# Lattice products cut into 64x64 tiles, two rounds a tile pair, with ordering products and five accumulators

## The chip, the cores and the metric

The kernel runs on one core of a Trainium2 chip. The metric is the device time of one execution in microseconds (us). The reference's work on an input of 32 images with 8 channels of 256x256 is done in one launch.

## What is computed

The reference normalises the input in groups, runs a block of three small networks on it, adds the result to the input, normalises again and adds a quantised 3x3 convolution. Cut to what matters here, the first layer is:

```python
drive = x                                  # normalised input, 8 channels
grid = drive
for _ in range(15):                        # STEPS: the lattice
    mapped = 3.9 * grid * (1.0 - grid)
    local = conv3x3_per_channel(mapped, K_local)
    physics = 0.7 * mapped + 0.3 * local
    grid = 0.85 * physics + 0.15 * drive
cml_out = clip(grid, 0.0001, 0.9999)
h = relu(conv3x3(x, Wp, bp))               # 128 hidden channels
nca_out = sigmoid(conv1x1(h, Wu, bu))
g = sigmoid(conv1x1(relu(conv3x3(concat(x, cml_out, nca_out), Wg1, bg1)), Wg2, bg2))
out = g * cml_out + (1 - g) * nca_out
```

The lattice loop is what the change touches. Each step of it is a 3x3 convolution within a channel, so a step needs the whole plane of the step before, and 15 steps follow each other.

## The kernel before, in words

All images are taken in 8 groups of four. For a group, three pieces of work run in the first layer: the lattice (`lattice`), the hidden network (`nca`), and the gate of the group before (`gate`); the normalisation of the next group (`normalise`) is mixed in as well. After the last group's gate comes the second layer, the quantised convolution (L982 to L1040), which the change leaves alone.

**Layout of the lattice.** A plane of 256x256 is put on 128 partitions as four column phases of 32 rows: partition = 32 x phase + row within the tile. A tile has 32 rows, of which 28 are its own; 9 tiles cover an image, and two images stand side by side in one buffer, so a buffer has 18 tiles, with 64 columns a phase (NJ). The loop over tiles takes 6 at a time, so a step has three tile ranges `i`. Each group of four images makes two buffers, `s` = 0 and 1. There are two layouts, "a" and "b", which differ by a shift of the phases: a step takes one buffer from a to b (65 columns a tile, so products with 390 columns) and the other from b to a (64 columns, 384). They change roles at every step. The buffers are `m_a` and `m_b`; the drive is in `d_a` and `d_b`.

**The product of a step.** For each range `i` and each of the two buffers, three fp32 products with weights of 128 rows and 64 columns (L511) make one accumulator `pt`: two write one half of its partitions each from the buffer's own columns (`own`), and the third adds to the second half's sum what the neighbouring columns give (`beside`, one column aside). The two buffers' products alternate, one writing the low and one the high half of the partitions. The six products of a range are called a tile pair's here: three rounds of two products. Of the three weights of a buffer two hold zeros in one half of their 128 rows, so with the rows cut in halves four blocks of 64x64 hold all that is not zero.

**What follows a product.** VectorE adds the drive (`gt`, L519, which frees the accumulator), and makes `mapped` of the next step (L524), written into the other layout's buffer. GpSimd clears the two outer columns after a step from a to b (L528). After a step from b to a, the halo rows between tiles are copied by DMA (`exchange`, L474 and L475): for the first image after range `i` = 1, for the second after `i` = 2. SyncE issues these, and `background(3)` issues three more DMAs of loads and stores for other channels after each range.

**The other products.** `hidden` (L591) multiplies two row blocks of 48 partitions by 128 columns of weights into two accumulators `ph`, with ScalarE's `h` (L601) reading them. `place` (L608) makes `acc` from `h`. The gate has `pa` (L795) and `pg` (L758).

**Accumulators.** PSUM has eight banks here: `ps_c` has six buffers under the tag "pt", which go round among pt, ph, pg and a few one-column sums, and `ps_a` two for acc and pa. A buffer is waited for when its reader of six requests before hasn't finished.

**Order.** TensorE's order is the program's (`manual_schedule` for PE). `together` (after the definition of `lattice`, `nca` and `gate`) alternates the lattice, which yields a cost of 5.91 after each step, with the others' pieces, by their share of the total costs (T_LATTICE = 8 * 45 * 1.97, T_NCA, T_GATE, T_PREP), so a lattice step is followed by a few pieces of filler. VectorE, ScalarE, GpSimd and SyncE are ordered by a scheduler.

Of the kernel before, what the change touches and what calls it, by code (L numbers as in the profile page):

```python
# [31 lines left out]
F32 = mybir.dt.float32  # L32
# [6 lines left out]
PSUM = bass.MemoryType.PSUM  # L39

P = 128
# [16 lines left out]
NJ = W // 4  # L58
# [55 lines left out]
def kernel(  # L114
# [17 lines left out]
    V, S, G, T = nc.vector, nc.scalar, nc.gpsimd, nc.tensor  # L132
# [13 lines left out]
    lw = cp.tile([P, C, 3, P], F32, name="lw")  # L146
# [6 lines left out]
    qw = cp.tile([P, 3, P], BF16, name="qw")  # L153
# [19 lines left out]
    with tc.tile_pool(name="prep", bufs=1) as pp, tc.tile_pool(name="prep2", bufs=2) as pp2:  # L173
# [24 lines left out]
        for t, n, w in (  # L198
# [3 lines left out]
            k = 64 if w == W else 43  # L202
# [63 lines left out]
    with ExitStack() as one:  # L266
# [4 lines left out]
        pool = lambda name, bufs, **kw: one.enter_context(  # L271
            tc.tile_pool(name=name, bufs=bufs, reuse_waits="tile", **kw)
        )
        hp, xp, sp2, gp, bp2 = pool("hp", 12), pool("xp", 4), pool("sp2", 1), pool("gp", 3), pool("bp2", 2)
        st, imp, wk, wk1, np_ = pool("st", 2), pool("imp", 3), pool("wk", 2), pool("wk1", 2), pool("np", 1)
        ps_c, ps_a = pool("ps_c", 6, space=PSUM), pool("ps_a", 2, space=PSUM)

        fixed = lambda shape, name, dt=F32: np_.tile(shape, dt, name=name)
        hi, lo = fixed([P, 2, 2, PW], "hi", F32R), fixed([P, 2, 2, PW], "lo", F32R)
# [10 lines left out]
        m_a = [fixed([P, TU, NJ + 2], f"m_a{i}") for i in range(2)]  # L290
        m_b = [fixed([P, TU, NJ + 1], f"m_b{i}") for i in range(2)]
# [100 lines left out]

        NG = B // GB
        ready = set()

        def lattice(g):


            def load(u):


                c, out, dmas = u % C, [], []
                assert all((u // C * GB + i, c // 2) in ready for i in range(GB))
                for s in range(2):
                    i = (2 * u + s) % 4
                    da, db = d_a[i], d_b[i]
                    for k in range(2):
                        src = xq_s[((u // C) * GB + 2 * s + k) % NBUF]
                        ts = slice(NT * k, NT * k + NT)
                        for i in range(8):  # L410
                            q, odd = divmod(i, 2)
                            dims = [[2 * W, 16], [TSTEP * W, NT], [1, NJ]]
                            dmas.append(
                                (
                                    da[16 * i : 16 * i + 16, ts, :],
                                    dram_ap(src, (c * H + odd) * W + q * NJ, dims),
                                )
                            )
                    dmas.append((db[R4:, :, 0:NJ], da[: P - R4, :, :]))
                    dmas.append((db[:R4, :, 1 : 1 + NJ], da[P - R4 :, :, :]))  # L420
                    out.append((da, db))
                return out, dmas

            def begin(ds, ts):

                (da, _), (_, db) = ds
                V.scalar_tensor_tensor(
                    m_a[0][:, ts, 1 : 1 + NJ], da[:, ts, :], 1.0, da[:, ts, :], ALU.subtract, ALU.mult
                )
                V.scalar_tensor_tensor(m_b[1][:, ts, :], db[:, ts, :], 1.0, db[:, ts, :], ALU.subtract, ALU.mult)  # L430
                for t in (*ds[0], *ds[1]):
                    S.activation(t[:, ts, :], t[:, ts, :], AF.Copy, scale=BETA)
# [29 lines left out]
            def background(n):  # L462
                for _ in range(min(n, len(later))):
                    nc.sync.dma_start(*later.pop(0))  # L464
                    n -= 1
                    issued[0] += 1
                if g == 0 and units.keys() - {0}:
                    for _ in range(min(n, len(borders))):
                        nc.sync.dma_start(*borders.pop(0))

            def exchange(t, k):

                above, below = slice(NT * k, NT * k + NT - 1), slice(NT * k + 1, NT * k + NT)
                nc.sync.dma_start(t[0::16, below, :], t[14::16, above, :])  # L474
                nc.sync.dma_start(t[15::16, above, :], t[1::16, below, :])  # L475

            tiles = [slice(6 * i, 6 * i + 6) for i in range(3)]
# [6 lines left out]
            for c in range(C):  # L484
                u = g * C + c
                ds = units[u]
                for step in range(STEPS):
                    if step == 7 and u + 1 < NG * C:
                        units[u + 1], dmas = load(u + 1)
                        later.extend(dmas)  # L490
                    if step == STEPS - 1:
                        background(len(later))
                    for i, ts in enumerate(tiles):

                        jobs = []
                        for s in range(2):
                            a2b = (step + s) % 2 == 0
                            n = NJ + 1 if a2b else NJ
                            pt = ps_c.tile([P, 512], F32, name="pt", tag="pt")
                            jobs.append((s, a2b, n, pt[:, : 6 * n].rearrange("p (t j) -> p t j", j=n)))  # L500

                        for part in range(3):
                            for s, a2b, n, pt in jobs:
                                own = m_a[s][:, ts, 1 : 2 + NJ] if a2b else m_b[s][:, ts, 0:NJ]
                                beside = m_a[s][:, ts, 0 : 1 + NJ] if a2b else m_b[s][:, ts, 1 : 1 + NJ]
                                low = a2b == (part != 1)
                                half = slice(0, 64) if low else slice(64, P)
                                k = 2 if part == 2 else 0 if a2b else 1  # L510
                                T.matmul(  # L511
                                    pt[half], lw[:, c, k, half], beside if part == 2 else own,
                                    start=part < 2, stop=part > 0,
                                )
                        for s, a2b, n, pt in jobs:
                            gt = gp.tile([P, 6 * (NJ + 1)], F32, name="gt", tag="gt")
                            gt = gt[:, : 6 * n].rearrange("p (t j) -> p t j", j=n)
                            d = ds[s][1 if a2b else 0]
                            V.scalar_tensor_tensor(gt, pt, FLOOR, d[:, ts, :], ALU.max, ALU.add)  # L519
                            if step == STEPS - 1:  # L520
                                V.tensor_scalar(d[:, ts, :], gt, 0.0001, 1.0 - 0.0001, ALU.max, ALU.min)
                                continue
                            to = m_b[s][:, ts, :] if a2b else m_a[s][:, ts, 1 : 1 + NJ]
                            V.scalar_tensor_tensor(to, gt, 1.0, gt, ALU.subtract, ALU.mult)  # L524
                            if a2b:

                                edge = m_b[s][:, ts, 0 : NJ + 1 : NJ]
                                G.tensor_tensor(  # L528
                                    edge, edge, junk.unsqueeze(1).to_broadcast([P, 6, 2]), ALU.mult
                                )  # L530
                        for s, a2b, n, pt in jobs:
                            for k in range(2):
                                if i != k + 1:
                                    continue
                                if step == STEPS - 1:
                                    b = g * GB + 2 * s + k
                                    later.extend(store(b, c, "b" if a2b else "a", ds[s][1 if a2b else 0], k))
                                elif not a2b:
                                    exchange(m_a[s], k)
                        if step == STEPS - 1 and u + 1 in units:  # L540
                            begin(units[u + 1], ts)
                        background(3)
                    yield 5.91
# [392 lines left out]
    with ExitStack() as two:  # L936
# [92 lines left out]
        for b in range(B + 1):  # L1029
            if b < B:  # L1030
                y = ys[b]
                ts = [scaled(b, y, h) for h in range(2)]
                for h in range(2):
                    quantised(b, ts[h], h)
            if last:
                i, os_ = last
# [9 lines left out]
            if done:  # L1046
                i, os_ = done
# [48 lines left out]
```

## Time and profile before

| | |
|---|---|
| median of three runs | 13871.5 us (13864.75 to 13885.28) |
| span of the profiled execution | 13862.1 us |
| its own time beside its span | not given apart; the median is 9.4 us over the span |
| lattice products on TensorE (L511) | 86 to 12930 us in the span |
| TensorE, VectorE, ScalarE, GpSimd busy | 95%, 59%, 29%, 18% |
| L511, mean of one record | 496 and 491 ns, two records for an fp32 product |
| mean granted clock of TensorE | 0.975 |

The profile is of one execution. A group line gives the line of the kernel, the engine, the operation, what it writes and reads, the shapes, the count, then the busy time in us and the mean of one in ns, and the idle time ahead. Shapes of a product are rows*columns of the weights and then partitions x elements. Records of products overlap, and their ends are modelled: a record of 491 ns is longer than the 0.32 us from one start to the next. PEld is the weight load, PE the product. The chain that ended last is the list of work, followed back from the last instruction, that had to be waited for; in order of time it is a list of start, length and what ran.

### The profile page before, as it was taken

The page shows a single profiled execution, that of the slowest core. Times are in us where ns is not written, and L with a number is a line of the kernel's source. Part 1 is how long each engine was busy: PE and PEld are TensorE (multiplying, and loading weights), DVE is VectorE, ACT ScalarE, POOL GpSimd, SP SyncE. Part 2 cuts the span into 40 slices and gives each one's busy share as a digit, 9 for nine tenths or more (in the row PEclk, how much of TensorE's full clock was granted, in tenths as well). Part 3 has the DMA queues.
Part 4 walks back from the last instruction along what each step waited for, and adds up shares of the span by engine and source line. Part 5 has one row for each costly group of instructions (what it writes and reads, how often), then busy time and mean ns, then how long its engine had stood idle before and what let it go on. Part 6 is the DMA issues. An engine that isn't in the chain of part 4 may idle for free.

```text
span 13862.1 us, 229831 instructions
## 1 busy us (share of the span) xinstructions
PE 13134.4 (95%) x81840; PEld 6403.4 (46%) x81840; DVE 8176.8 (59%) x16402; ACT 4028.2 (29%) x6274; POOL 2454.7 (18%) x4278
## 2 busy tenths in 40 slices
PE   4899999999999999999999999999999999999964
PEld 2445544444444444444444444444444444444322
DVE  5555565566655565555655565555655555555577
ACT  2233223232322223322323223222223222222123
POOL 1001111121111211111111111112111111111310
PEclk8999999999999999999999999999999999999986
DMA  6444444444444444444444444444444433333368
GB/s 152 96 97 99 96 104 112 101 98 101 111 99 103 109 93 108 108 104 93 107 106 101 102 104 103 102 106 108 94 108 110 100 91 84 89 79 89 90 202 257
DMA packets 2287210, 1496.77 MB, mean 108 GB/s; under 512 B 1096576, under 2 KB 2257152, under 8 KB 2285952
## 3 DMA queue, kind: packets, MB, share of 16 engines
q1 hardware_dynamic: 2191360, 1392.13, 43.1%
q10 hardware_dynamic: 94720, 89.93, 2.1%
q8 instruction: 665, 10.90, 0.3%
q14 instruction: 465, 3.81, 0.1%
HBM read 866.48 MB, written 478.69 MB: 97 GB/s over the span
## 4 chain that ended last, share of the span: by engine, by line
PE 81%; DMA 8%; SPq 4%; DVE 3%; issue 1%; ACTq 1%; ACT 0%; POOL 0%; POOLq 0%; DVEq 0%
PE pt L511 36%; PE ph L591 20%; PE pa L795 16%; PE acc L608 7%; DMA yb<-y_s 2%; PE pg L758 2%; DMA im<-xp_s 1%; DVE gt L519 1%; ACTq L1021 1%; DMA m_a<-m_a 1%; DMA xb<-in_x_dram 1%; DMA xp_s<-lo 1%; SPq L464 1%; SPq L569 1%; DVE m_a L524 1%
## 5 line engine op out<-in xcount | busy, mean ns | idle before, releaser
L511 PE MATMUL pt<-m_a,lw 128*64 128x390 f32 x17280 | 5842.6, 496 | 162.0 <-DMA m_a<-m_a 103.3
L511 PE MATMUL pt<-m_b,lw 128*64 128x384 f32 x17280 | 5809.7, 491 | 18.9 <-DVE m_b L430 18.1
L601 ACT ACTIVATE h<-ph,bp_sb 128x512 f32<-128x512 f32 x4096 | 2581.8, 684 | 4845.8 <-PE ph L591 4772.4
L511 PEld LDWEIGHTS pt<-m_a,lw 128*64 128x64 f32 x17280 | 2302.2, 138 | 1795.4 <-issue 1597.2
L511 PEld LDWEIGHTS pt<-m_b,lw 128*64 128x64 f32 x17280 | 2310.1, 138 | 1638.4 <-issue 1522.3
L591 PE MATMUL ph<-im,wp_hi 48*128 48x512 f32 x12288 | 2685.1, 415 | 119.0 <-DMA im<-xp_s 59.4
L519 DVE SCALAR_TENSOR_TENSOR gt<-pt,d_b 128x390 f32<-128x390 f32 x2880 | 1609.3, 559 | 1820.8 <-PE pt L511 1818.2
L519 DVE SCALAR_TENSOR_TENSOR gt<-pt,d_a 128x384 f32<-128x384 f32 x2880 | 1584.1, 550 | 1837.4 <-PE pt L511 1836.7
L591 PE MATMUL ph<-im,wp_lo 48*128 48x512 f32 x12288 | 2569.9, 398 | 0.0
L528 POOL TENSOR_TENSOR m_b<-m_b,junk 128x12 f32<-128x12 f32 x2688 | 817.1, 304 | 8414.1 <-DVE m_b L524 7988.0
L591 PEld LDWEIGHTS ph<-im,wp_hi 48*128 48x128 f32 x12288 | 1312.0, 187 | 969.7 <-DVE m_a L524 180.7
L524 DVE SCALAR_TENSOR_TENSOR m_b<-gt 128x390 f32<-128x390 f32 x2688 | 1557.1, 579 | 46.4 <-DVE gt L519 0.9
L524 DVE SCALAR_TENSOR_TENSOR m_a<-gt 128x384 f32<-128x384 f32 x2688 | 1540.3, 573 | 18.0
L591 PEld LDWEIGHTS ph<-im,wp_lo 48*128 48x128 f32 x12288 | 1309.2, 188 | 218.6
L608 PE MATMUL acc<-h,wu_z 128*32 128x512 f32 x8320 | 1155.1, 598 | 6.1 <-ACT nca L626 5.5
L795 PE MATMUL pa<-cmb,gw 128*64 128x512 f32 (+1 forms) x3840 | 861.4, 580 | 15.5 <-POOL cmb L723 15.5
L795 PE MATMUL pa<-xnb,gw 128*64 128x512 f32 (+1 forms) x3840 | 847.8, 574 | 11.1 <-ACT r L812 11.1
L795 PE MATMUL pa<-nb,gw 128*64 128x512 f32 (+1 forms) x3840 | 847.2, 573 | 0.0
L762 DVE TENSOR_TENSOR gate<-gate,d 128x512 f32<-128x512 f32 x320 | 218.3, 682 | 823.0 <-ACT gate L760 805.0
L812 ACT ACTIVATE r<-pa,bv 128x512 f32<-128x512 f32 x320 | 213.1, 666 | 1650.4 <-PE pa L795 1650.4
L729 DVE TENSOR_SCALAR xnb<-xb,sc 128x256 f32<-128x256 f32 x608 | 305.0, 517 | 596.9 <-DMA xb<-in_x_dram 590.7
L760 ACT ACTIVATE gate<-pg,bv 128x512 f32<-128x512 f32 x320 | 213.2, 666 | 1519.1 <-PE pg L758 1508.1
(133 smaller groups left out, 7225.3 us busy)
## 6 DMA issues: line engine op xcount, KB each, us to landing
im<-xp_s SPq DMA_DIRECT2D x1152, 193.5 KB
im<-xp_s SPq DMA_DIRECT2D x1216, 96.8 KB
d_a<-xq_s SPq DMA_DIRECT2D x2048, 36.0 KB
nb<-nc_s SPq DMA_DIRECT2D x288, 256.0 KB
cq<-cm_s SPq DMA_DIRECT2D x288, 256.0 KB
xb<-in_x_dram SPq DMA_DIRECT2D x544, 128.0 KB
yb<-y_s ACTq DMA_DIRECT2D x28, 2432.0 KB
xp_s<-hi SPq DMA_DIRECT2D x256, 258.0 KB
```

What stands on the lines that cost most here:

```text
L511: T.matmul(pt[half], lw[:, c, k, half], beside if part == 2 else own, start=part < 2, stop=part > 0,)
L519: V.scalar_tensor_tensor(gt, pt, FLOOR, d[:, ts, :], ALU.max, ALU.add)
L524: V.scalar_tensor_tensor(to, gt, 1.0, gt, ALU.subtract, ALU.mult)
L528: G.tensor_tensor(edge, edge, junk.unsqueeze(1).to_broadcast([P, 6, 2]), ALU.mult)
L591: T.matmul(ph[:, :n].rearrange("p (h w) -> p h w", w=W), w[64 * i : 64 * i + 48, dx, :], rhs[:, :, dx : dx + W], start=(dx == 0 and w is w ...
L601: S.activation(h[:, :n], ph[:, :n], AF.Relu, bias=bp_sb)
L608: T.matmul(acc[32 * g : 32 * g + 32, :cols], wu_z[:, 24 - 8 * i : 56 - 8 * i], h, start=first, stop=last,)
L729: V.tensor_scalar(xnb[:, k, 1 : 1 + W], xb[:, k, :], sc[:, i : i + 1], sc[:, 1:2], ALU.subtract, ALU.mult,)
L758: T.matmul(pg[half, :cols], gw2[:, half], r1[:, :cols], start=True, stop=True)
L760: S.activation(gt[:, :cols], pg[:, :cols], AF.Sigmoid, bias=bv[:, 1:2])
L762: V.tensor_tensor(three(y), three(gt), d[:, :n, :], ALU.mult)
L795: T.matmul(three[half], gw[:, s * 3 + dx, half], t[:, :n, dx : dx + W], start=(i == 0), stop=(i == 8),)
```

## The change

The six products of a tile pair, each with 128 rows of weights, become eight with 64 rows and 64 columns: of each buffer's four 64x64 blocks. Two of a buffer's four make the first round (`first` is true, they start the sums in both halves of `pt`), two the second (they add). In each round, one buffer uses the blocks on the diagonal and the other the two beside it, so that the four products of a round use the four 64x64 tiles of the array. In the first round buffer 0 writes pt's low half from the low rows and the high half from the high rows, buffer 1 the reverse; in the second round they change. An accumulator is hence written from both row halves, in different rounds.

The rounds of the three tile pairs are ordered: pair 0 first, pair 1 first, pair 0 second, then pair 1 second, pair 2 first, pair 2 second. Between them stand products of one column, `fence`, in bf16 with weights of 64x64 from `qw`, into an eighth bank `mark` of a pool of one buffer (`ps_m`). In the built program each of them is a weight load and a product, and the product waits for TensorE's own semaphore, that is for the ordering product before it (the step's first one mostly needs no such wait). Five stand in each step; two of them follow each other ahead of pair 2's second round. The pool `ps_c` has five buffers in place of six.

In the built program TensorE has 23040 lattice products in place of 17280, and 4800 ordering products; what stands between the lattice's steps is the same as before. VectorE's operations are the same in number and shape; the scheduler orders them a little differently, since their inputs are due at other times.

```diff
-        ps_c, ps_a = pool("ps_c", 6, space=PSUM), pool("ps_a", 2, space=PSUM)
+        ps_c, ps_a = pool("ps_c", 5, space=PSUM), pool("ps_a", 2, space=PSUM)
+        ps_m = pool("ps_m", 1, space=PSUM)
...
+        LOW, HIGH = slice(0, 64), slice(64, P)
...
+                    def turn(i, first):
+                        if first:
+                            work[i] = [job(i, s) for s in range(2)]
+                        ts = tiles[i]
+                        for s, a2b, n, pt in work[i]:
+                            own = m_a[s][:, ts, 1 : 2 + NJ] if a2b else m_b[s][:, ts, 0:NJ]
+                            beside = m_a[s][:, ts, 0 : 1 + NJ] if a2b else m_b[s][:, ts, 1 : 1 + NJ]
+                            k = 0 if a2b else 1
+                            if (s == 0) == first:
+                                parts = ((LOW, LOW, k, own), (HIGH, HIGH, k, own))
+                            elif a2b:
+                                parts = ((LOW, HIGH, k, own), (HIGH, LOW, 2, beside))
+                            else:
+                                parts = ((HIGH, LOW, k, own), (LOW, HIGH, 2, beside))
+                            for src, dst, w, rhs in parts:
+                                T.matmul(
+                                    pt[dst], lw[src, c, w, dst], rhs[src], start=first, stop=not first
+                                )
+                    def fence():
+                        mark = ps_m.tile([P, 512], F32, name="mark", tag="mark")
+                        T.matmul(mark[HIGH, 0:1], qw[HIGH, 0, HIGH], qw[HIGH, 0, 0:1], start=True, stop=True)
+                    work = {}
+                    TURNS = (
+                        ((0, True), None, (1, True), None, (0, False)),
+                        (None, (1, False)),
+                        ((2, True), None, None, (2, False)),
+                    )
                     for i, ts in enumerate(tiles):
-                        jobs = []
-                        for s in range(2):
...
-                        for part in range(3):
-                            for s, a2b, n, pt in jobs:
...
-                                low = a2b == (part != 1)
-                                half = slice(0, 64) if low else slice(64, P)
-                                k = 2 if part == 2 else 0 if a2b else 1
-                                T.matmul(
-                                    pt[half], lw[:, c, k, half], beside if part == 2 else own,
-                                    start=part < 2, stop=part > 0,
-                                )
+                        for t in TURNS[i]:
+                            turn(*t) if t else fence()
+                        jobs = work[i]
                         for s, a2b, n, pt in jobs:
```

`job` allots an accumulator as the removed lines did. VectorE's, GpSimd's and SyncE's part of the loop stays as it is.

More of the change, by code (lines that the diff above doesn't have):

```diff
@@ L492, in lattice @@
                         background(len(later))
-                    for i, ts in enumerate(tiles):
-                        jobs = []
-                        for s in range(2):
[L497 to L500, printed above, removed]
-                        for part in range(3):
-                            for s, a2b, n, pt in jobs:
-                                own = m_a[s][:, ts, 1 : 2 + NJ] if a2b else m_b[s][:, ts, 0:NJ]
-                                beside = m_a[s][:, ts, 0 : 1 + NJ] if a2b else m_b[s][:, ts, 1 : 1 + NJ]
-                                low = a2b == (part != 1)
-                                half = slice(0, 64) if low else slice(64, P)
-                                k = 2 if part == 2 else 0 if a2b else 1
-                                T.matmul(
-                                    pt[half], lw[:, c, k, half], beside if part == 2 else own,
-                                    start=part < 2, stop=part > 0,
-                                )
@@ new lines, in job @@
+                    def job(i, s):
+                        a2b = (step + s) % 2 == 0
+                        n = NJ + 1 if a2b else NJ
+                        pt = ps_c.tile([P, 512], F32, name="pt", tag="pt")
+                        return s, a2b, n, pt[:, : 6 * n].rearrange("p (t j) -> p t j", j=n)
+                    def turn(i, first):
[16 more added lines that the diff above has]
+                                )
```

## The prediction

> **What bounds the kernel now.** I read the page's busy shares first, then the chain that ended last, then that chain in order of time in a stretch in the middle, then single products, then VectorE's timeline in the same stretch.
>
> ```profile
> PE 13134.4 (95%) x81840; PEld 6403.4 (46%) x81840; DVE 8176.8 (59%) x16402; ACT 4028.2 (29%) x6274; POOL 2454.7 (18%) x4278
> PE   4899999999999999999999999999999999999964
> PEclk8999999999999999999999999999999999999986
> PE pt L511 36%; PE ph L591 20%; PE pa L795 16%; PE acc L608 7%; DMA yb<-y_s 2%; PE pg L758 2%; DMA im<-xp_s 1%; DVE gt L519 1%; ACTq L1021 1%; DMA m_a<-m_a 1%; DMA xb<-in_x_dram 1%; DMA xp_s<-lo 1%; SPq L464 1%; SPq L569 1%; DVE m_a L524 1%
> L511 PE MATMUL pt<-m_a,lw 128*64 128x390 f32 x17280 | 5842.6, 496 | 162.0 <-DMA m_a<-m_a 103.3
> ```
>
> TensorE is busy in nine tenths of nearly every slice, at nearly full clock, and the largest piece of the chain is L511, the lattice product that the change rewrites. It ends at 12930 us; gate work of the last group and the second layer follow and are not touched.
>
> ```profile
> 5032.94 6.02 PE pt L511 x36
> 5038.96 2.58 PE pa L795 x12
> 5041.54 3.01 PE ph L591 x24
> 5044.54 2.73 PE pa L795 x12
> 5047.27 0.86 PE pg L758 x4
> 5048.13 5.86 PE pt L511 x33
> 5053.99 3.18 PE ph L591 x24
> 5057.16 1.85 PE acc L608 x16
> 5059.02 6.01 PE pt L511 x33
> ```
>
> In this stretch the chain never leaves TensorE: a lattice step of some 5.9 us, then filler products. So here a microsecond off TensorE is a microsecond off the time, until something else is late. From 86 to 12930 us there are 960 steps (8 groups, 8 channels, 15 steps), 13.4 us each.
>
> ```profile
> 5006.12 0.49 PE L511 MATMUL pt<-m_a,lw 128*64 128x390 f32 x1
> 5006.13 0.48 PE L511 MATMUL pt<-m_b,lw 128*64 128x384 f32 x1
> 5006.45 0.49 PE L511 MATMUL pt<-m_a,lw 128*64 128x390 f32 x1
> 5006.45 0.49 PE L511 MATMUL pt<-m_b,lw 128*64 128x384 f32 x1
> ```
>
> An fp32 product has two records. The two column halves start together, 10 ns apart, and again one slot of 0.323 us later: both run at once. A step is 3 tile pairs x 3 rounds x 2 records = 18 slots = 5.82 us.
>
> ```profile
> 5037.22 0.55 DVE L519 SCALAR_TENSOR_TENSOR gt<-pt,d_a 128x384 f32<-128x384 f32 x1
> 5037.68 0.56 DVE L519 SCALAR_TENSOR_TENSOR gt<-pt,d_b 128x390 f32<-128x390 f32 x1
> 5038.15 0.55 DVE L524 SCALAR_TENSOR_TENSOR m_a<-gt 128x384 f32<-128x384 f32 x1
> 5038.62 0.56 DVE L524 SCALAR_TENSOR_TENSOR m_b<-gt 128x390 f32<-128x390 f32 x1
> 5039.09 0.55 DVE L519 SCALAR_TENSOR_TENSOR gt<-pt,d_a 128x384 f32<-128x384 f32 x1
> ```
>
> VectorE takes an operation every 0.47 us, 1.87 us a tile pair, just under TensorE's 1.94. It reads the accumulators (gt) and so sets when they come free. This is the next bound.
>
> **What the Trainium skill says.** "TensorEngine Tiling (Array Packing)", section Key Properties: tiles run independently, and a change of tiling mode drains the engine. The trace agrees: two products of L795 follow each other 0.423 us apart, L608 (128*32) to L511 (128*64) takes 0.523, so a change costs 0.10 us. "TensorE: Matmul & The Clock Gate", Part 3: row and column tiling compose, 16 tiles of 32x32 measured 10.6 times as fast. The trace of before shows columns together (L511) and rows together (L591: pairs of 48-row products 0.235 us apart), not both at once. The same page, section on LDWEIGHTS: columns / 1.2 ns, 53 ns for 64; in the trace a tile's second load comes 0.055 us after its first. "PSUM — Partial Sum Buffer", section on bank collisions: two row tiles may not write one bank and quadrant at once. No run here shows it; I take it for the reason of the ordering products.
>
> **The change part by part.** Made against the span of 13862.1 us; the median of the runs, 13871.5, lies 9 us above it.
>
> Rounds. 12 of 18 slots remain: 3.88 us in place of 5.82, 1.94 saved, x 960 = 1863 us. This takes the slot as unchanged with four tiles. Bounds: 0.323 us (each partition is still read by two streams, loads overlap) and 0.65, if row halves take turns. L591 shows row halves at once, so I take 0.323.
>
> Single ordering products (three a step). Such a product is a one-column one in the tile of rows and columns 64 to 127. Its weights go in while the tile still works, but the tile's next load must wait until it starts: 0.055 us, taken as 0.06. It waits for the one before, a whole round (0.65 us) back, while a product is known to a waiter 0.2 us after its slot (first gt to last product's start: 0.527 in most steps, less 0.323), so that wait has ended. Lower bound 0; upper 0.35, if all four tiles drain. 3 x 0.06 = 0.18.
>
> Double ordering product ahead of tile pair 2's second round. The second waits for the first, and nothing of the lattice stands between; all of TensorE's queue stands behind it. 0.2 to completion, some 0.1 for the second, 0.06 for the reload, 0.05 for the restart: 0.4 (0.25 to 0.7). Together 0.58 a step, 557 us.
>
> Mode changes. Gate products (128*64) beside a lattice block shared its mode and no longer do. The order of the changed program's TensorE instructions has 404 steps that leave to them, and about as many enter: some 770 x 0.10 = 77 us. The filler and its place are otherwise the same in both programs.
>
> Five accumulators. Tile pair 2's second one is now pair 0's first. Pair 0 ends at 1.94 + 2 x 0.06 = 2.06 us; gt starts 0.2 later, and read and hand-over take 0.56 + 0.06: free at 2.88. It is wanted after pair 1's second round, 2.06 + 0.06 + 0.65 = 2.77. That is 0.11; but over the 960 steps, read off VectorE's and TensorE's timelines, the first gt starts 0.37 us later in the mean than in the median step (2.58 against 2.21; gate work in VectorE's queue). I take 0.35: 336 us. Left: 1863 - 557 - 77 - 336 = 893 us, 0.93 a step; the block is then some 4.9 us.
>
> The filler's accumulators. In 446 steps ph follows the lattice at once, mostly two pairs, four accumulators. Pair one's second is tile pair 1's first, pair two's second is tile pair 2's first. gt of tile pair 2 starts 8 operations after the first: 2.26 + 8 x 0.47 + 0.62 = 6.64, with the mean lag and other work some 7.2. Pair two is ready at 4.9 + 0.1 + 1.41 (six slots of 0.235) = 6.4. So 0.8 us is lost, 0.9 with pair one's short wait; before, with six, pair two wanted tile pair 1's and hardly waited. 446 x 0.9 = 400 us; about 100 of it are waits that the kernel had already (1/3 of the 0.4 us by which its 13.4 us a step exceed its products). Cost 300. In the 404 steps with gate products first (2.58 us on other accumulators) the wait is hidden. Without DVE's lag the cost would be half.
>
> The halo exchange. Its DMA lands 1.4 us after issue, two issues of 0.6 follow VectorE's last m_a: 2.2 us. m_a of tile pair 2 is done at about 8; the next step's pair 1 wants the halo at once after pair 0's first round (0.7 us in, not 1.94). So a step can't be under 9.5 us. Few are (those with one or two short filler pieces): a tenth, losing 1 us: 90 us. SyncE's queue, its issues the same, stays under 80% of the time.
>
> Sum: 893 - 300 - 90 = 503; 13862 - 503 + 9 = 13368, given as **13350**. VectorE, ScalarE and GpSimd do the same work.
>
> **The rivals.**
>
> No stalls: VectorE's lag is absorbed and the double product costs 0.25. Then 1863 - 77 - 0.43 x 960 = 1370 is the limit; with 150 for what remains, 12650. For it: VectorE is only 59% busy. Against: it can't start before pair 0's second round, now no earlier than before.
>
> Slower: every ordering product, not only the double, stops all four tiles. The place is the four stops of each step; the price 0.35 us (completion, reload, restart) for each single and 0.7 for the double, 1.75 a step in place of 0.58, 1120 us more. Some 260 of that hides in the waits for VectorE, which shrink. 13350 + 1120 - 260 = 14210. It decides from about 0.22 us a single product (0.16 more x 3 x 960 = 460, and the double's share). For it: the program waits on TensorE's own semaphore at each; tiles' mixing of fp32 and bf16 in this way is not in the trace. Against: a round lies between the waits.
>
> Swallowed: the PSUM waits eat all. Then TensorE's shorter block only ends earlier before the same VectorE release, in all steps: 0.93 - 0.9 of 960, about 13830. Against: gate-first steps.
>
> That the tiles don't overlap at all (slot 0.65) would be 2.0 us a step more, 15700; 3 in 100, within the slower case.
>
> **How the numbers follow.** Forecast (gain of 270 to 770 us: 13100 to 13600) 52%; no stalls 15%; swallowed 10%; slower 23%. Faster by over 0.2% (28 us, about what a measurement of this kernel tells from none): 52 + 15 + 6 = 73%; within 4%; slower 23%. The range 12700 to 14050 leaves out half of no stalls and half of slower.
>
> **What would show it.** Right: a lattice block of about 4.5 to 4.9 us; four products starting within some 20 ns and again 0.32 later; a gap of 0.4 us before the last round; TensorE waits at ph and pt on gt of VectorE, in ph-first steps; TensorE's share down. Wrong: slots over 0.4 us; gaps over 0.2 us at single ordering products; m_a's DMA as a large releaser.

## The result, and the profile after

The changed kernel takes **14399.4 us** in the median of four runs (14388.4 to 14417.7), beside 13874.7 for the kernel before on the same chip: a ratio of **1.0379** (95% interval 1.0364 to 1.0393). It is slower by 525 us; the prediction was 13350, with a range to 14050. The profiled execution spans 14402.9 us, at a mean granted clock of 0.942 (before 0.975). The lattice ends at 13468 us in place of 12930, so the whole difference lies in it.

Lines of the page after:

```profile
PE 12711.2 (88%) x98160; PEld 6266.2 (44%) x98160; DVE 8312.4 (58%) x16402; ACT 4032.7 (28%) x6274; POOL 2322.8 (16%) x4278
PE   4888899999999989899899999999899999999964
PEclk8889999999999999999999999999999999999987
PE 51%; DVE 19%; DMA 14%; SPq 8%; issue 5%; ACT 1%; ACTq 1%; POOL 1%; DVEq 0%; POOLq 0%
L521 PE MATMUL pt<-m_a,lw 64*64 64x390 f32 x23040 | 4553.5, 519 | 583.0 <-DVE gt L546 319.6
```

The engines' shares of the same chain in the kernel before:

```profile
PE 81%; DMA 8%; SPq 4%; DVE 3%; issue 1%; ACTq 1%; ACT 0%; POOL 0%; POOLq 0%; DVEq 0%
```

TensorE is busy 88% in place of 95%, and the chain that ended last is no longer mostly TensorE's: VectorE, DMA and SyncE's queue (SPq) hold 41% of it, where they held 15%. The lattice products now stand idle for VectorE's `gt` ahead of them (319.6 us for this half of them), where before the largest releaser was a DMA with 103.3 us.

TensorE's timeline of one lattice block with nothing late beside it (start, length, line, what, count):

```profile
5506.50 0.54 PE L521 MATMUL pt<-m_b,lw 64*64 64x384 f32 x2
5506.52 0.55 PE L521 MATMUL pt<-m_a,lw 64*64 64x390 f32 x2
5506.88 0.49 PE L521 MATMUL pt<-m_b,lw 64*64 64x384 f32 x2
5506.89 0.49 PE L521 MATMUL pt<-m_a,lw 64*64 64x390 f32 x2
...
5507.20 0.16 PE L530 MATMUL mark<-qw 64*64 64x1 bf16 x1
...
5507.91 0.16 PE L530 MATMUL mark<-qw 64*64 64x1 bf16 x1
...
5508.62 0.16 PE L530 MATMUL mark<-qw 64*64 64x1 bf16 x1
...
5509.98 0.51 PE L530 MATMUL mark<-qw 64*64 64x1 bf16 x2
5510.33 0.54 PE L521 MATMUL pt<-m_b,lw 64*64 64x384 f32 x2
...
5511.15 0.50 PE L618 MATMUL ph<-im,wp_hi 48*128 48x512 f32 x2
```

The four products of a round start within 20 ns and their second records follow after the usual slot: four tiles work at once. The single ordering products stand 0.71 us apart, which is two slots of 0.323 and 0.06. From the block's first product to one slot after its last product's start it takes 4.55 us here (the filler, with its change of mode, starts at 4.65); in the steps that half clock does not touch the median is 4.62 (743 steps), in place of 5.91 before. In its products, then, the change does what was forecast. In the mean over all 960 steps, waits included, the block takes 5.83 us in place of 6.06: most of that gain is lost inside the block itself.

What it loses shows in the chain in order of time, in a stretch in the middle (start, length, what; the short pieces are left out):

```profile
6010.54 1.85 PE acc L635 x16
6012.39 2.15 PE pt L521 x18
6014.56 0.57 DVE gt L546
6015.15 0.56 DVE m_a L551
6015.71 0.53 DVE gt L546 x2
6016.57 0.55 DVE m_b L551
6018.17 0.56 DVE m_b L551
6019.23 0.56 DVE m_a L551
6020.37 0.57 DVE m_b L551
6020.94 0.61 DVE gate L789
6021.57 0.70 DVE gate L790
6022.30 0.69 DVE st_a L798
6022.99 0.58 DVE mx L799
6023.57 0.59 DVE mn L800
6025.61 1.02 DVE gt L546 x2
```

In the stretch shown of the kernel before, the chain never left TensorE. Here it goes to VectorE at the first `gt` and stays there, and in its queue the gate's five operations (L789 to L800, 3.2 us) stand between the lattice's: the next `gt` comes after them, and pair 2's first round needs an accumulator that only pair 0's `gt` frees.

A longer case. TensorE's timeline, and VectorE's of the same time:

```profile
5484.36 1.00 PE L521 MATMUL pt<-m_a,lw 64*64 64x390 f32 x6
5492.77 0.91 PE L521 MATMUL pt<-m_b,lw 64*64 64x384 f32 x2 [7.41 <-DVE mv L324]
...
5497.36 0.63 PE L618 MATMUL ph<-im,wp_lo 48*128 48x512 f32 x2
5497.78 0.63 PE L618 MATMUL ph<-im,wp_hi 48*128 48x512 f32 x2
```

```profile
5488.26 0.41 DVE L756 TENSOR_SCALAR xnb<-xb,sc 128x256 f32<-128x256 f32 x1 [4.50 <-DMA xb<-in_x_dram]
...
5490.88 1.28 DVE L323 BATCH_NORM_STATS2 stats<-xr 128x6 f32<-128x512 f32 x2 [1.07 <-DMA xr<-in_x_dram]
5492.08 0.55 DVE L546 SCALAR_TENSOR_TENSOR gt<-pt,d_b 128x390 f32<-128x390 f32 x1
```

VectorE itself waits 4.50 us for a load of the gate (L756) and 1.07 for one of the next group's normalisation (L323), while `gt`, whose sum has long been there, stands behind both. TensorE is named as waiting for `mv`, which ended last; what it needs is `gt`, done at 5492.63. The stretches around it (us, their length, busy time of PE, PEld, DVE, ACT, POOL, granted clock, DMA share, GB/s):

```profile
5480.00:5484.00 4.00, 4.00 (x45) 2.72 (x45) 3.69 (x5) 2.53 (x4) 3.45 (x3) 1.00 0.85 227
...
5490.00:5495.00 5.00, 2.13 (x10) 0.63 (x14) 4.12 (x9) 0.00 (x0) 0.21 (x1) 0.50 1.08 192
5495.00:5500.00 5.00, 5.00 (x28) 3.25 (x22) 4.60 (x10) 1.13 (x2) 0.42 (x2) 0.50 0.05 17
5500.00:5503.00 3.00, 3.00 (x20) 1.10 (x20) 0.00 (x0) 1.40 (x3) 0.00 (x0) 0.57 0.62 180
5503.00:5506.00 3.00, 3.00 (x20) 0.77 (x12) 0.00 (x0) 0.00 (x0) 0.00 (x0) 1.00 0.03 5
```

After the wait TensorE runs at half its clock until about 5502.6, for some 10 us: the pairs at L618 follow each other every 0.43 us in place of 0.235. The Trainium skill, "TensorE: Matmul & The Clock Gate", section "HAM oscillation — how this bites in real kernels", has this as a rule, no idle gaps over about 3.4 us. The trace agrees only in part: the largest gap in the 3.4 us ahead of each of the 187 drops has a mean of 3.2 us, but more than half of these gaps are shorter than 3.4 (the median is 3.0), and a tenth are below 0.9.

All of this summed over the trace, from 400 us to the end of the lattice (us, but for the counts of gaps and drops; a gap is time in which no product's record runs; a drop is a change to half clock; the lag is the first `gt` of a step, counted from the step's first product, mean and median, over all steps; the block's median is that of the steps without half clock):

| kernel | lattice ends | TensorE idle | gaps over 1 us | drops | at half clock | lag of gt | block, median |
|---|---|---|---|---|---|---|---|
| before | 12930 | 237 | 69 | 42 | 218 | 2.58, 2.21 | 5.91 |
| after | 13468 | 1159 | 349 | 187 | 1198 | 3.40, 2.36 | 4.62 |

Idle time is up by 922 us, time at half clock by 980.

### The profile page after: what moved, and what is told of

Same layout as the page of the kernel before. It is cut to its first block, busy times and chain, and to the rows that moved or that the text cites. A ratio compares the mean times of both kernels' runs of the same rounds, so it can differ in the third digit from the quotient of the medians.

```text
span 14402.9 us, 260311 instructions
## 1 busy us (share of the span) xinstructions
PE 12711.2 (88%) x98160; PEld 6266.2 (44%) x98160; DVE 8312.4 (58%) x16402; ACT 4032.7 (28%) x6274; POOL 2322.8 (16%) x4278
## 4 chain that ended last, share of the span: by engine, by line
PE 51%; DVE 19%; DMA 14%; SPq 8%; issue 5%; ACT 1%; ACTq 1%; POOL 1%; DVEq 0%; POOLq 0%
PE pt L521 16%; PE ph L618 14%; PE pa L822 13%; DVE gt L546 8%; PE acc L635 6%; DVE m_b L551 4%; DMA xb<-in_x_dram 3%; DVE m_a L551 3%; DMA yb<-y_s 2%; SPq L596 2%; DMA im<-xp_s 2%; DMA xr<-in_x_dram 1%; PE pg L785 1%; SPq L466 1%; DMA m_a<-m_a 1%
## 5 line engine op out<-in xcount | busy, mean ns | idle before, releaser
L521 PE MATMUL pt<-m_a,lw 64*64 64x390 f32 x23040 | 4553.5, 519 | 583.0 <-DVE gt L546 319.6
L521 PE MATMUL pt<-m_b,lw 64*64 64x384 f32 x23040 | 4528.4, 510 | 222.6 <-DVE gt L546 126.8
L618 PE MATMUL ph<-im,wp_hi 48*128 48x512 f32 x12288 | 3055.9, 428 | 329.1 <-DVE gt L546 213.5
L618 PE MATMUL ph<-im,wp_lo 48*128 48x512 f32 x12288 | 2877.1, 412 | 0.0
L521 PEld LDWEIGHTS pt<-m_a,lw 64*64 64x64 f32 x23040 | 1636.0, 136 | 1878.2 <-issue 987.3
L521 PEld LDWEIGHTS pt<-m_b,lw 64*64 64x64 f32 x23040 | 1658.8, 136 | 1305.4 <-issue 978.1
L618 PEld LDWEIGHTS ph<-im,wp_hi 48*128 48x128 f32 x12288 | 1615.7, 193 | 1389.4 <-DVE gt L546 851.4
L618 PEld LDWEIGHTS ph<-im,wp_lo 48*128 48x128 f32 x12288 | 1619.8, 194 | 221.9
L551 DVE SCALAR_TENSOR_TENSOR m_b<-gt 128x390 f32<-128x390 f32 x2688 | 1562.7, 581 | 114.8 <-DVE gt L546 4.1
L551 DVE SCALAR_TENSOR_TENSOR m_a<-gt 128x384 f32<-128x384 f32 x2688 | 1561.1, 581 | 47.6
L530 PE MATMUL mark<-qw 64*64 64x1 bf16 x4800 | 793.8, 165 | 93.0
L756 DVE TENSOR_SCALAR xnb<-xb,sc 128x256 f32<-128x256 f32 x608 | 287.3, 481 | 776.7 <-DMA xb<-in_x_dram 766.6
L762 POOL TENSOR_TENSOR d<-cmb,nb 128x512 f32<-128x512 f32 x320 | 503.8, 1574 | 1089.3 <-DVE gate L789 908.4
```

The lines of the kernel that those rows point to most:

```text
L521: T.matmul(pt[dst], lw[src, c, w, dst], rhs[src], start=first, stop=not first)
L530: T.matmul(mark[HIGH, 0:1], qw[HIGH, 0, HIGH], qw[HIGH, 0, 0:1], start=True, stop=True)
L618: T.matmul(ph[:, :n].rearrange("p (h w) -> p h w", w=W), w[64 * i : 64 * i + 48, dx, :], rhs[:, :, dx : dx + W], start=(dx == 0 and w is w ...
L756: V.tensor_scalar(xnb[:, k, 1 : 1 + W], xb[:, k, :], sc[:, i : i + 1], sc[:, 1:2], ALU.subtract, ALU.mult,)
L762: G.tensor_tensor(d[:, :n, :], cmb[:, :n, 1 : 1 + W], nin, ALU.subtract)
```

## The experiments

The theory after the result: the products' saving is there, and VectorE's order gives it back; the rivals are the missing accumulator itself, the ordering products, and VectorE's amount of work in place of its order. Each ratio is to the kernel before, run on the same chip; from chip to chip the kernel before took 13849 to 13905 us, so a difference in us between runs on different chips is good to some 50 us.

**One accumulator fewer, in both kernels.** In the kernel before six become five; in the changed one five become four.

```diff
-        ps_c, ps_a = pool("ps_c", 6, space=PSUM), pool("ps_a", 2, space=PSUM)
+        ps_c, ps_a = pool("ps_c", 5, space=PSUM), pool("ps_a", 2, space=PSUM)
```

> The kernel before with five accumulators in place of six, nothing else. My theory (the changed kernel's TensorE waits for VectorE, because five accumulators come free only as fast as VectorE reads them, and the lumped waits bring its clock to half): in the kernel before a lattice block takes 5.8 us, longer than VectorE needs for two tile pairs, so five should cost little here, 50 to 200 us over the kernel before, under 1.5%; the cost comes with the shorter block. Rival (five accumulators alone are what costs): 500 us or more over the kernel before, about 14400 us, with TensorE waiting at ph and pt for gt.

Measured: 14019.0 us, 1.0118 (1.0103 to 1.0133).

> The changed kernel with four accumulators in place of five. If accumulators freed by VectorE are the bound, one fewer costs as much again or more: each pair of the filler waits for one more gt, 0.5 to 1 us a step, and pair 2's first round waits for two: 15000 to 15600 us, half-clock time doubled. If the ordering products' stops or VectorE's queue on DMA are the cause: 14400 to 14700.

Measured: 14997.9 us, 1.0826 (1.0808 to 1.0843), at the lower end of the range. TensorE's waits in it (line, releaser: us in total, times, longest):

```profile
PE pt L521 <- DVE gt L546: 704.0, 704, 6.6
```

The number of accumulators is a cause of its own: 170 us for the sixth where blocks are long, some 600 for the fifth where they are short. It does not carry the whole change: the old products with five accumulators are still 380 us faster than the new ones with five. What the sixth would be worth to the new products is not shown.

**The filler in two places.** So that pair 2 meets a VectorE that has caught up, half of the filler goes ahead of pair 2, after pair 1's last round, and half stays behind the block.

```diff
                         background(3)
-                    yield 5.91
+                        if i:
+                            yield 2.955
```

> The changed kernel with the filler put in two places of a step, after tile pair 1's second round and after tile pair 2's, instead of all after pair 2's. All products and ordering products stay. My theory: VectorE then has time to free accumulators before pair 2 asks for them; TensorE's idle time at pt and ph on gt (660 us in the changed kernel) falls to less than half and the half-clock time with it: 13500 to 13900 us. Rival (the ordering products' stops cost it): they all remain, so the time stays at 14300 to 14500. Rival (VectorE's queue is held by gate inputs still on their way by DMA): some gain, about 14200, since lags of several us remain.

Measured: 15202.5 us, 1.0975 (1.0959 to 1.0992); it lies 1300 us above the range that I expected. Its waits:

```profile
PE pt L521 <- DMA m_a<-m_a: 1122.6, 550, 11.2
...
PE pt L521 <- DVE gt L546: 51.3, 44, 5.5
```

The wait aimed at went, from 446 to 51 us (that of `ph` for `gt` rose, from 213 to 340). But with pair 2 later, its `m_a` and the halo DMA after it are later, and the next step, which has only half of the filler in between, waits for that: 187 us became 1123. Filler after the block covers VectorE's tail and the halo; it can't be moved ahead for nothing.

**One wait out of VectorE's queue.** `xnb` (L756), which waits for a load, goes to GpSimd, in both kernels.

```diff
-                V.tensor_scalar(
+                G.tensor_scalar(
                     xnb[:, k, 1 : 1 + W], xb[:, k, :], sc[:, i : i + 1], sc[:, 1:2],
```

> The changed kernel with the gate input's normalisation (xnb) moved from VectorE to GpSimd, so that VectorE's queue no longer stands behind a gate input on its way by DMA (767 us of VectorE idle in the changed kernel). If VectorE's lags come from that queue (rival): 13700 to 14000 us, TensorE idle on gt down by half. If they come from the pace of VectorE's own operations and five accumulators: 14250 to 14450, little changed. Ordering products as the cause: no change, 14400.

Measured: 14079.1 us, 1.0160 (1.0143 to 1.0177), between the two ranges: the queue is a part of it, not all.

> The kernel before with the gate input's normalisation (xnb) on GpSimd, as e3 did it to the changed kernel and gained 320 us. If VectorE's queue standing behind a gate input matters only once TensorE needs VectorE soon (my theory): no change, 13800 to 13900. If it holds up any kernel of this kind: 13550 to 13700.

Measured: 13867.9 us, 0.9973 (0.9964 to 0.9982). Some 320 us in the changed kernel, 37 in the one before: to take the same operation of 0.48 us out of VectorE's queue is worth eight times as much in the changed kernel.

**VectorE's work taken down.** Both kernels leave out, in all steps but the first of a channel, `mapped` of the next step (L524 before, L551 after) and the clearing of the outer columns; the lattice then multiplies the same `mapped` each time. L551 is 3124 of VectorE's 8312 us in the changed kernel.

```diff
                                 continue
+                            if step:
+                                continue
                             to = m_b[s][:, ts, :] if a2b else m_a[s][:, ts, 1 : 1 + NJ]
```

> The kernel before, with the operations that make the next step's input (m, on VectorE, and the edge's clearing on GpSimd) left out in all steps but the first of each channel, so later steps multiply the same values again; that takes away half of VectorE's lattice work and the wait for fresh values. The kernel before is bound by TensorE, so every theory expects little: 13700 to 13900 us.

Measured: 13587.5 us, 0.9776 (0.9762 to 0.9791), 110 us below the range: leaving this out was worth 317 us even there.

> The changed kernel with the same left out (m and the edge's clearing in all steps but the first of a channel). If the coupling to VectorE (its pace, five accumulators, the halo exchange behind it) and the clock that falls in the waits are what ate the gain, the products' own saving of about 0.9 us a step shows: 12800 to 13150 us, with the half-clock time near that of the kernel before (220 us). If ordering products or something else in TensorE's own stream costs it: 13900 to 14400.

Measured: 13288.4 us, 0.9560 (0.9545 to 0.9574), above the 12800 to 13150 that I expected. With a third of VectorE's busy time gone (5622 us are left of 8312) the new products win, but by 299 us only. Waits for `gt` are still there:

```profile
PE pt L521 <- DVE gt L546: 336.9, 194, 8.0
```

So it isn't only how much VectorE does: what stands ahead of `gt`, and waits there itself, remains. For the load of `xnb` alone VectorE still waits 755 us here, as in the changed kernel (767).

**Order alone.** VectorE takes the program's order in place of the scheduler's, and the two `gt` of a pair come ahead of its two `m`. Nothing else is edited, though the scheduler then orders the other queues a little differently too, GpSimd's most.

```diff
-        one.enter_context(tc.manual_schedule(engines={mybir.EngineType.PE}))
+        one.enter_context(tc.manual_schedule(engines={mybir.EngineType.PE, mybir.EngineType.DVE}))
...
-                        jobs = work[i]
+                        jobs, gts = work[i], []
...
                             V.scalar_tensor_tensor(gt, pt, FLOOR, d[:, ts, :], ALU.max, ALU.add)
+                            gts.append((s, a2b, n, gt, d))
+                        for s, a2b, n, gt, d in gts:
```

> The changed kernel with VectorE in the program's order and gt ahead of m, xnb left on VectorE: the half of e8 that isn't e3. If order and the queue behind gate inputs are two causes of about the same weight (e3 took 320 us, e8 another 380): 13950 to 14100 us. If the order alone is the cause and xnb only a part of it: 13700 to 13800. If the program's order puts xnb's wait for its DMA ahead of gt more often than the scheduler did: 14400 or more.

Measured: **13634.4 us, 0.9818** (0.9802 to 0.9835), below all of the ranges that I had named. The changed kernel with VectorE's order alone is 765 us faster than the changed kernel, and faster than the one before. VectorE's wait for the load of `xnb`, in the kernel before, in the changed one and in this run (us in total, times, longest):

```profile
DVE xnb L729 <- DMA xb<-in_x_dram: 590.7, 187, 16.6
DVE xnb L756 <- DMA xb<-in_x_dram: 766.6, 287, 18.5
DVE xnb L758 <- DMA xb<-in_x_dram: 15.1, 1, 15.1
```

The scheduler's order was hence not the same in the two kernels. In the changed one `xnb` stands five `gt` further ahead in VectorE's queue than in the one before (median of its 608 operations); in the program's order it stands twelve further behind than before. So a part of the loss may have come with the scheduler's new order; how much, no run shows. With `xnb` on GpSimd as well:

> The changed kernel with xnb on GpSimd as in e3, and VectorE's instructions in the program's order in place of the scheduler's, the two gt of a tile pair ahead of its two m. Accumulators then come free without gate work or normalisation being put ahead of them by a scheduler's guess of times. If VectorE's lag behind TensorE is a matter of that order, TensorE's idle time on gt falls by half and the clock's with it: 13300 to 13750 us, under the kernel before. If the five accumulators and VectorE's pace alone set it: 14000 to 14150, as e3. If the program's order makes VectorE wait for inputs that the scheduler moved away from: 14200 or more.

Measured: 13695.1 us, 0.9857 (0.9842 to 0.9871). And the same two edits in the kernel before:

> The kernel before with e8's edits (xnb on GpSimd, VectorE in the program's order, gt ahead of m), its lattice products and six accumulators kept. My theory: TensorE bounds this kernel and seldom waits for VectorE, so order changes little: 13750 to 13950 us. Then e8's 13695 owes its lead to the lattice products. Rival (the order helps every kernel alike): 13200 to 13400.

Measured: 13811.4 us, 0.9948 (0.9933 to 0.9963). With the move of `xnb`, the order is worth 704 us in the changed kernel and 77 in the one before. This is what tells the theory from its rivals: accumulators, ordering products and the amount of VectorE's work are the same in the changed kernel and in the run of order alone. By the ratios, `xnb` on GpSimd now loses some 50 us; it helped only the scheduler's order.

**The gate's operations behind the lattice step.** The gate's five operations on VectorE are kept in a list and run after the next lattice step.

```diff
                         background(3)
+                    catch_up()
                     yield 5.91
...
-                V.tensor_tensor(three(y), three(gt), d[:, :n, :], ALU.mult)
...
+                behind.append(lambda: vector(p, n, cols, three, y, d, f))
```

> e8 (the changed kernel, xnb on GpSimd, VectorE in the program's order, gt ahead of m) with the gate's five VectorE operations put behind the next lattice step's, where in e8 they stand ahead of it whenever a gate product comes just before a lattice step (3.5 us of VectorE, seen on e8's chain). If TensorE's remaining waits on gt come from gate work ahead of gt: 13350 to 13600 us, with TensorE's idle time and half-clock time down again. If what remains is the halo exchange and the filler's accumulators: 13650 to 13750, as e8.

Measured, with the order and `xnb` on GpSimd: 13525.2 us, 0.9743 (0.9728 to 0.9757).

> The kernel before with e9's edits (e10's, and the gate's operations put behind the next lattice step's). My theory: again 13750 to 13950 us, and e9 under it by 250 us or more. Rival (order helps alike): 13200 or less, under e9.

Measured, the same in the kernel before: 13757.4 us, 0.9909 (0.9894 to 0.9924). This pair is the fair comparison of the products: with the same VectorE edits and on the same chip, the new ones are 232 us or 1.7% ahead, where I had expected 250 or more.

> The changed kernel with VectorE in the program's order, gt ahead of m, the gate's operations behind the next lattice step's, and xnb left on VectorE (e9 without its move). e12 was 61 us under e8, so the move to GpSimd seems to cost once the order is right. If so: 13420 to 13500 us, the best version. If xnb on VectorE hinders once gate work is out of the way: 13550 to 13650, above e9's 13525.

Measured, the order and the list, with `xnb` left on VectorE: **13490.1 us, 0.9713** (0.9696 to 0.9729), the fastest that computes the whole: 2.9% below the kernel before and 909 us below the changed one. Of the 2.9%, about 0.9 is what the order and the list give the kernel before (there with `xnb` on GpSimd). Its page and its waits:

```profile
PE 12337.5 (91%) x98160; PEld 6292.8 (47%) x98160; DVE 7945.5 (59%) x16402; ACT 4028.0 (30%) x6274; POOL 2533.2 (19%) x4278
PE   4888899999999999999999999999999999999964
```

```profile
PE pt L527 <- DMA m_a<-m_a: 239.3, 154, 8.2
PE pt L1052 <- ACT ob L1057: 234.6, 27, 11.7
PE pa L834 <- DVE xnb L765: 111.4, 33, 17.1
...
PE ph L627 <- ACT h L637: 65.5, 28, 4.4
```

The instructions are as many as in the changed kernel; the waits for `gt` are no longer among the seven longest. What is left most is the halo's DMA, then the gate's product for `xnb` (L1052 is the second layer's).

> e13 with four accumulators in place of five. With the scheduler's order of VectorE, four cost 600 us more than five (e4). If the number of accumulators is a cause of its own, the cost is the same with the right order, 500 us or more over e13. If it costs only because VectorE was late, 200 us or less.

Measured, that version with four accumulators: 14028.7 us, 1.0098 (1.0082 to 1.0115). One accumulator fewer still costs 540 us, so order and number of accumulators are two causes and don't replace each other. The cost lies in the block, whose median goes from 4.62 to 5.08 us, while TensorE's idle time hardly moves (639 and 618 us): waits too short to show as gaps, as I read it. Six beside the ordering products' bank were not tried: with `ps_a` all eight banks are taken.

The same sums over these traces:

| kernel | lattice ends | TensorE idle | gaps over 1 us | drops | at half clock | lag of gt | block, median |
|---|---|---|---|---|---|---|---|
| xnb on GpSimd | 13159 | 991 | 310 | 142 | 911 | 3.18, 2.31 | 4.62 |
| order alone | 12684 | 721 | 255 | 83 | 495 | 2.96, 2.24 | 4.62 |
| order and list | 12550 | 639 | 177 | 90 | 512 | 2.76, 2.24 | 4.62 |
| order and list, four accumulators | 13088 | 618 | 159 | 96 | 546 | 2.79, 2.24 | 5.08 |

From the changed kernel to each of the first three, the products are the same. If half of the time at half clock is lost, the change in idle time plus half that at half clock should give the change in the lattice's end: -312, -790 and -863 us against -309, -784 and -918. So by this account the slow clock cost the changed kernel up to 600 us, 490 more than the kernel before. It remains an estimate. The account says -865 for the changed kernel without `mapped`, where the end moved by -1103; and from the kernel before to the changed one, with 1238 us saved in the blocks' median, it says +174, where the end moved by +538. No run took the clock's share by itself.

## Why the prediction was wrong, step by step

**Rounds, ordering products, modes: right.** Forecast 1.94 - 0.58 = 1.36 us a step off the block; the medians give 1.29, or 1238 us against 1306. Slots stayed at 0.323 us; a single ordering product costs 0.06 as taken; the double one's two products start 0.41 us apart, and all five together cost 0.65 a step (1.94 less 1.29), against 0.58. A change of mode takes 0.10 (0.522 against 0.422 from product to product), as before. The rival that every ordering product stops all tiles, which gave 14210, was near the time for a mechanism that isn't there.

**Five accumulators: the step that failed.** The term charged 0.35 us a step, 336 us. Measured, the changed kernel's block is 1.21 us longer in the mean than in its median (5.83 against 4.62), where before it was 0.15: 1.06 us a step more, some 1020 us in all. At most some 210 of it can be the clock's, half of the 427 us by which the time at half clock inside the blocks went up (104 to 531). I read the lag of the first `gt` in the kernel before, 0.37 us in the mean over its median, and charged 0.35 to every step. Two things were wrong with that. The lag doesn't carry over: in the changed kernel the mean is 1.04 us above the median, and the scheduler's order is a part of that: in the program's order it is 0.72, with the list 0.52. The rest may be lateness that a step hands to the next; no run shows it apart. And it isn't spread out: the median step has almost none, and a tenth of the steps start `gt` over 3.9 us later than the median step. The recorded waits for `gt` at the lattice's products are 446 us over 189 waits, 2.4 us each, not 0.35 in each of 960.

**What a long wait brings: not in the sum at all.** "VectorE, ScalarE and GpSimd do the same work" was right and beside the point, and the clock has no term. Step by step against the kernel before, the 718 steps with no half clock in either kernel gain 244 us, where my 0.52 a step gives 376. In the 217 steps that half clock touches in the changed kernel, 862 us are lost, where the sum had a gain of 114. (The other 25 steps gain 80.) Of the miss of 1041 us, 976 lie in those 217 steps. They hold 1324 us at half clock (the first 400 us of the span included), against 233 in the same steps of the kernel before, so at most half of the difference, 545 us, is the clock's; the rest I take for the waits themselves.

**The filler's accumulators: too high, by the waits on record.** 400 us were taken for waits at `ph`; 394 waits with 213 us are there (before: 48 with 44), 0.54 each in place of 0.9. The halo: 90 us added were taken, the waits for m_a's DMA rose by 84, from 103 to 187.

**The bound.** "A microsecond off TensorE is a microsecond off the time, until something else is late": VectorE was named as the next bound by its pace, 1.87 us a pair against 1.94, and "swallowed", at 13830, had this mechanism. What I didn't price is that VectorE's lag cost the kernel before little: straightening its queue out (with `xnb` on GpSimd, without and with the list) gains 77 and 131 us there, and 704 and 874 in the changed one. The signs named as "right" (block of 4.5 to 4.9 us, met by its median and not its mean; four products within 20 ns, waits on `gt`) are all in the trace, and the time is still on the other side: none of them measured how long the waits were. With VectorE in order and the list, the same products give 13490. That this lies inside the 13100 to 13600 of the forecast is luck: 131 us of such edits help the old products too, and the new ones are 232 us ahead with both put right, not the 503 of the sum.

**What stays open.** How much of the loss is the clock's and how much the waits', since no run held the one and changed the other; what share the scheduler's new order of VectorE had in it; what the new products do with six accumulators, and what they do without ordering products: that would leave the writes of two row halves to one accumulator unordered, and wasn't tried.

## What to carry to other kernels

When an engine with slack feeds the one that sets the time, read the tail of its lag and not its mean, and look at what stands ahead of the needed operation in its queue: here waits for unrelated loads and five gate operations, which cost the kernel before little, cost more than the products' saving once these were fast. A change elsewhere can also move what a scheduler puts ahead of it, so compare the two queues. Before a block is shortened or an accumulator taken away, put the operations that free accumulators first in that queue; with that done in both kernels, the new products came out 1.7% ahead in place of 3.8% behind. And price a wait of some microseconds on TensorE by what follows it at half clock as well.

## What the runs showed of the hardware

Four fp32 products with 64x64 weights in the four tiles run fully at once: a slot of 0.323 us for 390 columns, as two 128x64 ones had. A one-column bf16 product in between costs 0.06 us while the tiles go on; two that depend on each other start 0.41 us apart. After gaps of some microseconds the granted clock was 0.50, and pairs at L618 took 0.43 us in place of 0.235 for some 10 us after the wait in the stretch shown.
